# Router on rows that are not normalized, and a row copy shared by two engines

## The chip, the core and the metric

The kernel runs on one core of one Trainium2 chip. The metric is the device time of one execution in microseconds; the time given for a kernel is the median of its runs. All data are float32, and a float32 matmul shows as two matmul records in the trace.

## The reference

One layer of a perceiver: cross-attention of 8 x 64 tokens of width 512 on a context of 1601 rows, then a linear-attention block with an MLP, then a mixture of eight experts of which each token uses two. Each block works on layer-normalized rows and adds to the residual `x`. The part that matters here is the last block:

```python
x = x + _L0_ffn_ref(_layernorm(x, axis=-1), w_router, w0, w1, wo)

# in _L0_ffn_ref, x being the normalized rows, t tokens
router_logits = x @ w_router
top_w, top_i = jax.lax.top_k(router_logits, K)          # K = 2 of 8
top_w = jax.nn.softmax(top_w, axis=-1)
gating = zeros((t, e)).at[arange(t)[:, None], top_i].add(top_w)
for ei in range(e):
    hmid = silu(x @ w0[ei]) * (x @ w1[ei])
    out = out + gating[:, ei:ei + 1] * (hmid @ wo[ei])
```

The layer norm is (x - mean) / sqrt(var + 1e-5), with no learned scale.

## The kernel before

The 512 tokens lie as four tiles (t = 0 to 3) of 128 rows. The order of the instructions on each engine is the order in which the program states them, and each engine's queue, the DMA issues in it included, is worked off in that order. Matmul outputs go to PSUM banks of 128 x 512 from two pools of four: `mm_bank` for work that is emptied at once, `acc_bank` for sums that last. A bank is taken again in turn, when its last reader is done.

Stages: cross-attention, linear attention, MLP, routing, experts. What the change touches begins at the end of the linear attention's output. `hidden(f, tokens)` (L765) makes one block of 128 columns of the MLP's first layer; `turn_h2(t)` (L731) transposes a tile of its input, and its four evacuations take turns between DVE and ACT. The second MLP matmul is `mlp_out(t, f, hid)` (L791), one matmul of 128 x 512 that adds block f of 16 to the sum of tile t. For the first eight blocks all four tiles are done together; the last eight (`HELD`) are kept back, so that each tile can be finished by itself. `last_chunks(t, part)` (L842) issues some of these eight for one tile. They are the work that stands between the steps of the routing, which is done one tile behind:

- `finish(t)` (L826): DVE adds the sum to the residual `xs`, takes mean and variance (L830, L832), ACT takes the square root (L834), DVE its reciprocal (L835) and the normalized rows `mn` (L836). ACT's queue then stores `mn` in DRAM (L839), POOL's stores `xs` as the start of the output (L840).
- `turn_m(t)` (L848): TensorE transposes the four 128 x 128 blocks of `mn`, ACT copies the bank to `m_t` (L853).
- `route(t)` (L855): four matmuls of 128 x 8 for the logits (L859), which DVE copies (L863); then the two largest, their places, and one-hot rows `hot` and `member`.
- `rank_tile(t)` (L884): a matmul over the tokens before counts each token's place in its expert; DVE makes `rank` (L890) and `onehot` (L894), a 128 x 128 selection of the rows for expert 0.
- `first_rows(t)` (L896): four matmuls add the selected rows, already transposed, of tile t to one bank, `first_bank`.
- `count_tile(t)` (L876) keeps the running count of members; `tabulate(t)` (L908) is a chain of small DVE operations ending in `spot`, by which POOL writes a table in DRAM with two indirect DMAs (L928).

The loop at L940 goes over t = 1 to 3 and puts the steps of tile t - 1 between the last chunks of tile t. After it come the steps of tile 3, then ACT copies `first_bank` to `xg_t0` (L959), the rows of the first expert's first tile. DVE takes the count and the last two tabulations, one matmul sums the counts (L966), DVE copies them (L968), and the gates follow from the two largest logits (L971 to L981): exp of the difference, a reciprocal, and a product with the one-hot rows. ACT stores the gates beside the rows in DRAM (L982), POOL loads the table (L984).

The experts follow. For each, TensorE makes the hidden rows (L1081), DVE and ACT apply the gate function (L1044, L1046), TensorE transposes and multiplies back (L1052, L1089), ACT scales by the gate, and POOL adds the rows to the output by an indirect DMA (L1062). The rows of all tiles but the very first are fetched by POOL from DRAM (L1017), by places that DVE works out from the loaded table (L1007 to L1011). An expert with more than 128 rows takes a small second group; one with many more takes a further whole tile. Weights stream through a ring of twelve buffers of 1 MB by DMAs on SP's queue (L192).

```python
    for t in range(1, NT):
        last_chunks(t, range(0, 4))
        turn_m(t - 1)
        last_chunks(t, range(4, 5))
        route(t - 1)
        last_chunks(t, range(5, 7))
        rank_tile(t - 1)
        last_chunks(t, range(7, HELD))
        finish(t)
        first_rows(t - 1)
```

Of the kernel before, what the change touches and what calls it, by code (L numbers as in the profile page):

```python
# [15 lines left out]
F32 = mybir.dt.float32  # L16
AF = mybir.ActivationFunctionType
ALU = mybir.AluOpType
AX = mybir.AxisListType

P = 128
B, S, D = 8, 64, 512
LK = 1601
NT = B * S // P
KC = D // P
# [7 lines left out]
NE, FE = 8, 1024  # L33
# [5 lines left out]
HELD = 8  # L39
# [7 lines left out]
def perceiver_kernel(  # L47
# [22 lines left out]
    nc = tc.nc  # L70
# [4 lines left out]
    small = ctx.enter_context(tc.tile_pool(name="small", bufs=2))  # L75
# [6 lines left out]
    def mm_bank(name):  # L82
        return ps.tile([P, 512], F32, tag="mm", name=name)

    def acc_bank(name):
        return ps.tile([P, 512], F32, tag="acc", name=name)
# [10 lines left out]
    xs = resid.tile([P, NT, D], F32, name="xs")  # L97
    for t in range(0, NT, 2):
        nc.sync.dma_start(xs[:, t : t + 2, :], x[:, t : t + 2, :])
    moe = ctx.enter_context(tc.tile_pool(name="moe", bufs=1))  # L100
# [109 lines left out]
    ident = const.tile([P, P], F32, name="ident")  # L210
# [8 lines left out]
    router = col[:, 4 * KC + FF // P :].rearrange("p (c e) -> p c e", c=KC)  # L219
# [21 lines left out]
    ones = const.tile([P, P], F32, name="ones")  # L241
# [523 lines left out]
    def hidden(f, tokens):  # L765
# [4 lines left out]
        for c in range(KC):  # L770
# [5 lines left out]
                stop=(c == KC - 1),  # L776
            )

    hid_banks = {}

    hidden(0, slice(0, 3 * P))
# [9 lines left out]
    def mlp_out(t, f, hid):  # L791
        nc.tensor.matmul(  # L792
            acc[t],
            hid[:, t * P : (t + 1) * P],
            need("w2", f // 4)[:, f % 4, :],
            start=(f == 0),
            stop=(f == FF // P - 1),
        )
# [17 lines left out]
    mn = mlp.tile([P, NT, D + NE], F32, tag="mn", name="mn")  # L816
# [6 lines left out]
    member = moe.tile(full, F32, name="member")  # L823
    members = moe.tile(full, F32, name="members")

    def finish(t):  # L826

        nc.vector.tensor_tensor(xs[:, t, :], acc[t], xs[:, t, :], ALU.add)  # L828
        st = small.tile([P, 6], F32, tag="st", name=f"st_m_{t}")
        nc.vector.bn_stats(st, xs[:, t, :])  # L830
        mv = small.tile([P, 2], F32, tag="mv1", name=f"mv_m_{t}")
        nc.vector.bn_aggr(mv, st)  # L832
        rstd = small.tile([P, 1], F32, tag="rstd1", name=f"rstd_m_{t}")
        nc.scalar.activation(rstd, mv[:, 1:2], AF.Sqrt, bias=eps)  # L834
        nc.vector.reciprocal(rstd, rstd)  # L835
        nc.vector.tensor_scalar(  # L836
            mn[:, t, :D], xs[:, t, :], mv[:, 0:1], rstd, ALU.subtract, ALU.mult
        )
        nc.scalar.dma_start(mn_dram[t * P : (t + 1) * P, :D], mn[:, t, :D])  # L839
        nc.gpsimd.dma_start(out[t * P : (t + 1) * P, :], xs[:, t, :])  # L840

    def last_chunks(t, part):  # L842
        for f in part:
            mlp_out(t, nf - HELD + f, hids[nf - HELD + f])
# [3 lines left out]
    def turn_m(t):  # L848
        bank = mm_bank(f"tr_m_{t}")
        for c in range(KC):  # L850
            nc.tensor.transpose(bank[:, c * P : (c + 1) * P], mn[:, t, c * P : (c + 1) * P], ident)
        m_ts[t] = mlp2.tile([P, KC, P], F32, tag="mT", name=f"m_t_{t}")
        nc.scalar.copy(m_ts[t].rearrange("p c q -> p (c q)"), bank)  # L853

    def route(t):  # L855

        bank = mm_bank(f"router_{t}")
        for c in range(KC):
            nc.tensor.matmul(  # L859
                bank[:, :NE], m_ts[t][:, c, :], router[:, c, :], start=(c == 0), stop=(c == KC - 1)  # L860
            )
        logits = small.tile([P, NE], F32, tag="logits", name=f"logits_{t}")
        nc.vector.tensor_copy(logits, bank[:, :NE])  # L863
        nc.vector.max(out=top[:, t, :], in_=logits)
        where = small.tile([P, NE], mybir.dt.uint32, tag="where", name=f"where_{t}")
        nc.vector.max_index(out=where, in_max=top[:, t, :], in_values=logits)
        nc.vector.tensor_copy(chosen[:, t, :], where[:, :2])
        nc.vector.tensor_tensor(
            hot[:, t, :, :],
            enum[:, None, :].to_broadcast([P, 2, NE]),  # L870
            chosen[:, t, :, None].to_broadcast([P, 2, NE]),
            ALU.is_equal,
        )
        nc.vector.tensor_tensor(member[:, t, :], hot[:, t, 0, :], hot[:, t, 1, :], ALU.add)

    def count_tile(t):  # L876
        if t == 0:
            nc.vector.tensor_copy(members[:, 0, :], member[:, 0, :])
        else:
            nc.vector.tensor_tensor(members[:, t, :], members[:, t - 1, :], member[:, t, :], ALU.add)  # L880
# [3 lines left out]
    def rank_tile(t):  # L884

        bank = mm_bank(f"rank_{t}")
        if t > 0:
            nc.tensor.matmul(bank[:, :NE], ones, members[:, t - 1, :], start=True, stop=False)
        nc.tensor.matmul(bank[:, :NE], earlier, member[:, t, :], start=(t == 0), stop=True)
        nc.vector.scalar_tensor_tensor(  # L890
            rank[:, t, :], bank[:, :NE], 1.0, member[:, t, :], ALU.add, ALU.mult
        )
        onehots[t] = mlp2.tile([P, P], F32, tag="onehot", name=f"onehot_{t}")
        nc.vector.tensor_scalar(onehots[t], slot[:, :P], rank[:, t, 0:1], None, ALU.is_equal)  # L894

    def first_rows(t):  # L896

        for c in range(KC):
            nc.tensor.matmul(
                first_bank[:, c * P : (c + 1) * P],  # L900
                mn[:, t, c * P : (c + 1) * P],
                onehots[t],
                start=(t == 0 and c == 0),
                stop=(t == NT - 1),
                skip_group_check=True,
            )

    def tabulate(t):  # L908

        r = small.tile([P, 2], F32, tag="r", name=f"r_{t}")  # L910
        for k in range(2):
            mine = small.tile([P, NE], F32, tag="which", name=f"mine_{t}_{k}")
            nc.vector.scalar_tensor_tensor(
                mine, hot[:, t, k, :], 1.0, rank[:, t, :], ALU.mult, ALU.mult, accum_out=r[:, k : k + 1]
            )
        over = small.tile([P, 2], F32, tag="over", name=f"over_{t}")
        nc.vector.tensor_scalar(over, r, float(P), None, ALU.is_gt)
        for i in range(2, NI):
            nc.vector.scalar_tensor_tensor(over, r, float(i * P), over, ALU.is_gt, ALU.add)

        at = small.tile([P, 2], F32, tag="at", name=f"at_{t}")
        nc.vector.tensor_scalar(at, r, 32.0, -32.0, ALU.mult, ALU.add)
        nc.vector.scalar_tensor_tensor(at, chosen[:, t, :], 4.0, at, ALU.mult, ALU.add)
        nc.vector.scalar_tensor_tensor(
            spot[:, t, :], over, float(1 - P * NE * NI), at, ALU.mult, ALU.add
        )
        for k in range(2):
            nc.gpsimd.indirect_dma_start(  # L928
                out=table.rearrange("p k two -> (p k) two"),
                out_offset=bass.IndirectOffsetOnAxis(ap=spot[:, t, k : k + 1], axis=0),  # L930
                in_=named[:, t, :],
                in_offset=None,
                bounds_check=P * NE * NI - 1,
                oob_is_err=True,
            )

    last_chunks(0, range(HELD))
    finish(0)
    first_bank = acc_bank("first_rows")
    for t in range(1, NT):  # L940

        last_chunks(t, range(0, 4))
        turn_m(t - 1)
        last_chunks(t, range(4, 5))
        route(t - 1)
        last_chunks(t, range(5, 7))
        rank_tile(t - 1)
        last_chunks(t, range(7, HELD))
        finish(t)
        first_rows(t - 1)  # L950
        if t > 1:
            tabulate(t - 2)
        count_tile(t - 1)
    turn_m(NT - 1)
    route(NT - 1)
    rank_tile(NT - 1)
    first_rows(NT - 1)
    xg_t0 = moe.tile([P, KC, P], F32, name="xgT_first")
    nc.scalar.copy(xg_t0.rearrange("p c q -> p (c q)"), first_bank)  # L959
    count_tile(NT - 1)  # L960
    for t in range(NT - 2, NT):
        tabulate(t)
# [2 lines left out]
    bank = mm_bank("counts")  # L965
# [3 lines left out]

    e2 = moe.tile([P, NT], F32, name="e2")  # L970
    nc.vector.tensor_tensor(e2, top[:, :, 1], top[:, :, 0], ALU.subtract)  # L971
    nc.scalar.activation(e2, e2, AF.Exp)
    r1 = moe.tile([P, NT], F32, name="r1")
    nc.vector.tensor_scalar_add(r1, e2, 1.0)
# [17 lines left out]
    if True:  # L992
# [150 lines left out]
        if True:  # L1143
# [24 lines left out]
            flat = "p e i -> p (e i)"  # L1168
# [243 lines left out]
```

## Time and profile before

| what | us |
|---|---|
| median of three runs | 684.81 (684.4 to 684.9) |
| profiled execution | 685.44 |
| its span, first to last instruction | 683.7 |
| second MLP matmul (L792), 128 records, busy | 58.8 |
| last add of the MLP's sum (L828) starts | 424.42 |
| first expert matmul (L1081) starts | 435.91 |
| last scatter to the output (L1062) starts | 673.40 |

The profile gives times from the span's start. A row of the timeline is start, length, engine, line, operation, output and inputs, and in brackets how long the engine had been idle and what ended that. "PEld" is the load of weights into the array, which runs beside a matmul; "ACTq" and "SPq" are the queues' own instructions, such as the issue of a DMA. The end of a matmul is modelled: matmuls of 128 x 512 take 0.59 in the trace but follow each other every 0.43. A table by stage gives, for a stretch of time, each engine's busy time and the share of full clock that TensorE was granted.

### The profile page before, as it was taken

To read this page: it belongs to the slowest core of one execution; us is meant where nothing else is said; L and a number is where in the kernel's file an instruction comes from. 1 tells how busy PE (TensorE), PEld (TensorE's weight loads), DVE (VectorE), ACT (ScalarE), POOL (GpSimd) and SP (SyncE) were. 2 spreads that over 40 slices of the span, in tenths; PEclk is the share of its full clock that TensorE was granted. 3 is DMA by queue.
4 is the path that set the end of the run, shared out by engine and by line. 5 is a ranking of instruction groups with operands and counts; after the bars stand their busy time and mean duration, and the time that the engine had idled before them with its cause. 6 is when DMAs were issued, how large, how long until landed. Compare 5 with 4: busy or idle time off the path is not lost. (4 is left out here: it accounts for less than half of the span.)

```text
span 683.7 us, 6217 instructions
## 1 busy us (share of the span) xinstructions
PE 638.9 (93%) x2376; PEld 296.2 (43%) x2376; DVE 179.1 (26%) x403; ACT 128.2 (19%) x240; POOL 61.7 (9%) x81
## 2 busy tenths in 40 slices
PE   4998989799999999999999998898999999989993
PEld 3643434244444444445444455543444344434441
DVE  4011323132228687670000035310311101110100
ACT  2241223220132121122011200211111111111110
POOL 2000000000000000041000002331012202120000
PEclk9999999999999999999999999699999999999998
DMA  8999999999601103021311323127397595694711
GB/s 328 418 420 385 418 385 413 370 367 422 232 13 62 62 0 124 1 69 55 112 62 73 106 79 126 61 61 265 136 390 257 199 357 175 233 348 175 283 17 18
DMA packets 24222, 138.04 MB, mean 202 GB/s; under 512 B 4164, under 2 KB 4164, under 8 KB 11896
## 3 DMA queue, kind: packets, MB, share of 16 engines
q1 hardware_dynamic: 20056, 129.90, 49.0%
q0 software_dynamic: 3024, 6.58, 4.3%
q10 hardware_dynamic: 1104, 1.07, 0.4%
q8 instruction: 23, 0.38, 0.2%
q14 instruction: 15, 0.12, 0.1%
HBM read 132.56 MB, written 4.97 MB: 201 GB/s over the span
## 5 line engine op out<-in xcount | busy, mean ns | idle before, releaser
L1081 PE MATMUL up<-e_up,xgT 128*128 128x512 f32 x224 | 100.2, 595 | 1.2 <-PEq L1310 1.2
L1081 PEld LDWEIGHTS up<-e_up,xgT 128*128 128x128 f32 x224 | 40.9, 190 | 50.4 <-issue 50.4
L1089 PE MATMUL y<-e_wo,hidT 128*128 128x512 f32 x128 | 61.0, 599 | 0.0
L792 PE MATMUL mlp<-w,hid_sb 128*128 128x512 f32 x128 | 58.8, 597 | 0.0
L1046 DVE TENSOR_TENSOR mid<-up,act 128x256 f32<-128x256 f32 x35 | 14.9, 425 | 164.2 <-ACT act L1044 159.7
L771 PE MATMUL hid<-v_sb,w 128*128 128x512 f32 (+2 forms) x144 | 56.6, 545 | 0.0
L472 PE MATMUL av<-ctx,eT 128*64 128x512 f32 x192 | 48.4, 617 | 7.3 <-DMA ctx<-in_ctx_dram 6.5
L423 PE MATMUL sc<-ctxT,pw_t 128*64 128x401 f32 (+1 forms) x256 | 48.1, 501 | 0.7 <-DMA ctxT<-in_ctx_T_dram 0.7
L771 PEld LDWEIGHTS hid<-v_sb,w 128*128 128x128 f32 x144 | 26.2, 190 | 29.1 <-issue 27.3
L792 PEld LDWEIGHTS mlp<-w,hid_sb 128*128 128x128 f32 x128 | 23.4, 190 | 24.9 <-issue 24.9
L1044 ACT ACTIVATE act<-up 128x256 f32<-128x256 f32 x35 | 13.4, 383 | 104.5 <-PE up L1081 95.7
L786 POOL TENSOR_TENSOR xin<-xin,b_bc 128x512 f32<-128x512 f32 x4 | 5.1, 1263 | 295.3 <-DVE rstd_h L728 291.1
L423 PEld LDWEIGHTS sc<-ctxT,pw_t 128*64 128x64 f32 x256 | 20.3, 136 | 26.3 <-issue 22.9
L1062 POOL DMA_INDIRECT out_dram<-y_sb,dst_late x11 | 16.8, 1529 | 161.1 <-ACTq L1310 103.7
L1089 PEld LDWEIGHTS y<-e_wo,hidT 128*128 128x128 f32 x128 | 22.4, 190 | 19.5 <-issue 19.1
L595 PE MATMUL wk<-h_t,wk 128*128 128x512 f32 x64 | 29.5, 604 | 0.0
L595 PE MATMUL wq<-h_t,wq 128*128 128x512 f32 x64 | 29.4, 602 | 0.0
L532 PE MATMUL v<-wv,h_t 128*128 128x512 f32 x64 | 28.7, 597 | 0.6 <-DVE h_t L519 0.6
L472 PEld LDWEIGHTS av<-ctx,eT 128*64 128x64 f32 x192 | 13.9, 140 | 35.3 <-issue 24.6
L691 PE MATMUL wo<-wo,a_t 128*128 128x512 f32 x64 | 28.6, 597 | 0.0
L671 DVE RECIPROCAL rden<-rden 128x512 f32<-128x512 f32 x8 | 26.8, 3354 | 0.3
L828 DVE TENSOR_TENSOR xs<-mlp,xs 128x512 f32<-128x512 f32 x4 | 2.8, 692 | 87.3 <-PE mlp L792 87.3
(230 smaller groups left out, 653.1 us busy)
## 6 DMA issues: line engine op xcount, KB each, us to landing
e_up<-in_L_ffn_up_dram SPq DMA_DIRECT2D x32, 1024.0 KB, 7.9
ctx<-in_ctx_dram SPq DMA_DIRECT2D x24, 1024.0 KB, 17.4
ctxT<-in_ctx_T_dram SPq DMA_DIRECT2D x24, 802.0 KB, 15.7
e_wo<-in_L_ffn_wo_dram SPq DMA_DIRECT2D x16, 1024.0 KB, 10.0
w<-in_L_attn_w_dram SPq DMA_DIRECT2D x8, 1024.0 KB, 11.7
ctxT<-in_ctx_T_dram SPq DMA_DIRECT2D x8, 796.0 KB, 16.7
big_up<-in_L_ffn_up_dram SPq DMA_DIRECT2D x4, 1024.0 KB, 7.9
wv<-in_L_attn_wv_dram SPq DMA_DIRECT2D x2, 1024.0 KB, 13.0
```

Of the source, the lines that this page charges most:

```text
L423: nc.tensor.matmul(sc[h * S : (h + 1) * S, :width], pw_t[:, c, (2 * t + h) * S : (2 * t + h + 1) * S], keys[h][:, c, :], start=(c == 0), s ...
L472: nc.tensor.matmul(av[h * S : (h + 1) * S, :], e_t[:, 4 * g + j, h * S : (h + 1) * S], rows[h][:, j, :], start=(g == 0 and j == 0), stop=F ...
L532: nc.tensor.matmul(bank, h_t[:, c, t * P : (t + 1) * P], wv_n[:, c, :], start=(c == 0), stop=(c == KC - 1))
L595: nc.tensor.matmul(bank, w[:, c, (j % 4) * P : (j % 4 + 1) * P], h_t[:, c, :], start=(c == 0), stop=(c == KC - 1),)
L671: nc.vector.reciprocal(rden, rden)
L691: nc.tensor.matmul(wo_banks[t], a_t[:, j, t * P : (t + 1) * P], wo_r[j // 4][:, j % 4, :], start=(j == 0), stop=(j == nj - 1),)
L771: nc.tensor.matmul(hid_banks[f][:, tokens], w[:, c, (f % 4) * P : (f % 4 + 1) * P], h2_t[:, c, tokens], start=(c == 0), stop=(c == KC - 1),)
L792: nc.tensor.matmul(acc[t], hid[:, t * P : (t + 1) * P], need("w2", f // 4)[:, f % 4, :], start=(f == 0), stop=(f == FF // P - 1),)
L1046: nc.vector.tensor_tensor(hid, bank[:, FQ:], act, ALU.mult)
L1062: nc.gpsimd.indirect_dma_start(out=out, out_offset=bass.IndirectOffsetOnAxis(ap=dst[:n, :], axis=0), in_=y_sb[:n, :], in_offset=None, boun ...
L1081: nc.tensor.matmul(bank, xg_t[:, c, :], up_of[q][:, c, :], start=(c == 0), stop=(c == KC - 1))
L1089: nc.tensor.matmul(y, h_t[:, j, :], w[:, 2 * (q % 2) + j, :], start=(q + j == 0), stop=(q + j == NQ))
```

## The change

Mean and scale of the layer norm are taken out of the router's path. With m the mean and s the reciprocal deviation of a row, the normalized row times the router's weights is s * (row @ w - m * sum(w)). The sums of the router's columns are made once, by matmuls with a matrix of ones ahead of `hidden(0)`, and copied by DVE. `turn_m` transposes `xs` instead of `mn`. The logits are `router_sums * (-m) + row @ w`, without s: since s is positive, the order of a row's logits is the same, and s is multiplied into the difference of the two largest ahead of the exponential. `finish` keeps -m in `neg_mean` and s in `rstds`, for all tiles.

The order changes, too. In the loop, `turn_m` comes after two chunks instead of four, `route` after one more, `rank_tile` after two more, and three are left before `finish`. `first_rows(2)` moves out of the loop: two of its four chunks stand ahead of the last tile's transposes and two behind. The copy of `first_bank` is cut into halves of 128 x 256, one on ACT and one on DVE, the latter ahead of `count_tile` and the last tabulations on that engine.

```diff
--- before.py
+++ after.py
@@ -776,6 +776,12 @@
                 stop=(c == KC - 1),
             )
 
+
+    bank = mm_bank("router_sums")
+    for c in range(KC):
+        nc.tensor.matmul(bank[:, :NE], ones, router[:, c, :], start=(c == 0), stop=(c == KC - 1))
+    router_sums = moe.tile([P, NE], F32, name="router_sums")
+    nc.vector.tensor_copy(router_sums, bank[:, :NE])
     hid_banks = {}
 
     hidden(0, slice(0, 3 * P))
@@ -823,6 +829,9 @@
     member = moe.tile(full, F32, name="member")
     members = moe.tile(full, F32, name="members")
 
+    neg_mean = moe.tile([P, NT], F32, name="neg_mean")
+    rstds = moe.tile([P, NT], F32, name="rstds")
+
     def finish(t):
 
         nc.vector.tensor_tensor(xs[:, t, :], acc[t], xs[:, t, :], ALU.add)
@@ -830,7 +839,8 @@
         nc.vector.bn_stats(st, xs[:, t, :])
         mv = small.tile([P, 2], F32, tag="mv1", name=f"mv_m_{t}")
         nc.vector.bn_aggr(mv, st)
-        rstd = small.tile([P, 1], F32, tag="rstd1", name=f"rstd_m_{t}")
+        nc.vector.tensor_scalar(neg_mean[:, t : t + 1], mv[:, 0:1], -1.0, None, ALU.mult)
+        rstd = rstds[:, t : t + 1]
         nc.scalar.activation(rstd, mv[:, 1:2], AF.Sqrt, bias=eps)
         nc.vector.reciprocal(rstd, rstd)
         nc.vector.tensor_scalar(
@@ -848,11 +858,12 @@
     def turn_m(t):
         bank = mm_bank(f"tr_m_{t}")
         for c in range(KC):
-            nc.tensor.transpose(bank[:, c * P : (c + 1) * P], mn[:, t, c * P : (c + 1) * P], ident)
+            nc.tensor.transpose(bank[:, c * P : (c + 1) * P], xs[:, t, c * P : (c + 1) * P], ident)
         m_ts[t] = mlp2.tile([P, KC, P], F32, tag="mT", name=f"m_t_{t}")
         nc.scalar.copy(m_ts[t].rearrange("p c q -> p (c q)"), bank)
 
     def route(t):
+
 
         bank = mm_bank(f"router_{t}")
         for c in range(KC):
@@ -860,7 +871,9 @@
                 bank[:, :NE], m_ts[t][:, c, :], router[:, c, :], start=(c == 0), stop=(c == KC - 1)
             )
         logits = small.tile([P, NE], F32, tag="logits", name=f"logits_{t}")
-        nc.vector.tensor_copy(logits, bank[:, :NE])
+        nc.vector.scalar_tensor_tensor(
+            logits, router_sums, neg_mean[:, t : t + 1], bank[:, :NE], ALU.mult, ALU.add
+        )
         nc.vector.max(out=top[:, t, :], in_=logits)
         where = small.tile([P, NE], mybir.dt.uint32, tag="where", name=f"where_{t}")
         nc.vector.max_index(out=where, in_max=top[:, t, :], in_values=logits)
@@ -893,9 +906,9 @@
         onehots[t] = mlp2.tile([P, P], F32, tag="onehot", name=f"onehot_{t}")
         nc.vector.tensor_scalar(onehots[t], slot[:, :P], rank[:, t, 0:1], None, ALU.is_equal)
 
-    def first_rows(t):
-
-        for c in range(KC):
+    def first_rows(t, chunks=range(KC)):
+
+        for c in chunks:
             nc.tensor.matmul(
                 first_bank[:, c * P : (c + 1) * P],
                 mn[:, t, c * P : (c + 1) * P],
@@ -939,24 +952,29 @@
     first_bank = acc_bank("first_rows")
     for t in range(1, NT):
 
-        last_chunks(t, range(0, 4))
+        last_chunks(t, range(0, 2))
         turn_m(t - 1)
-        last_chunks(t, range(4, 5))
+        last_chunks(t, range(2, 3))
         route(t - 1)
-        last_chunks(t, range(5, 7))
+        last_chunks(t, range(3, 5))
         rank_tile(t - 1)
-        last_chunks(t, range(7, HELD))
+        last_chunks(t, range(5, HELD))
         finish(t)
-        first_rows(t - 1)
+        if t < NT - 1:
+            first_rows(t - 1)
         if t > 1:
             tabulate(t - 2)
         count_tile(t - 1)
+    first_rows(NT - 2, range(0, 2))
     turn_m(NT - 1)
+    first_rows(NT - 2, range(2, KC))
     route(NT - 1)
     rank_tile(NT - 1)
     first_rows(NT - 1)
     xg_t0 = moe.tile([P, KC, P], F32, name="xgT_first")
-    nc.scalar.copy(xg_t0.rearrange("p c q -> p (c q)"), first_bank)
+    flat = "p c q -> p (c q)"
+    nc.scalar.copy(xg_t0[:, :2, :].rearrange(flat), first_bank[:, : 2 * P])
+    nc.vector.tensor_copy(xg_t0[:, 2:, :].rearrange(flat), first_bank[:, 2 * P :])
     count_tile(NT - 1)
     for t in range(NT - 2, NT):
         tabulate(t)
@@ -969,6 +987,7 @@
 
     e2 = moe.tile([P, NT], F32, name="e2")
     nc.vector.tensor_tensor(e2, top[:, :, 1], top[:, :, 0], ALU.subtract)
+    nc.vector.tensor_tensor(e2, e2, rstds, ALU.mult)
     nc.scalar.activation(e2, e2, AF.Exp)
     r1 = moe.tile([P, NT], F32, name="r1")
     nc.vector.tensor_scalar_add(r1, e2, 1.0)
```

## What was predicted

> **What bounds the kernel now.** I read the page's busy table and slices first, then the table of busy time by stage, then the timeline of the last router tile, engine by engine.
>
> ```profile
> PE 638.9 (93%) x2376; PEld 296.2 (43%) x2376; DVE 179.1 (26%) x403; ACT 128.2 (19%) x240; POOL 61.7 (9%) x81
> PEclk9999999999999999999999999699999999999998
> ```
>
> TensorE is busy 93% of the span, and one slice of the clock row (the 6) is slow. The stage table finds it (start:end in us, its length, then busy time of PE, PEld, DVE, ACT, POOL, then clock, DMA share, GB/s):
>
> ```profile
> 412.00:420.00 8.00, 8.00 (x32) 4.27 (x30) 4.58 (x23) 0.80 (x2) 1.52 (x2) 1.00 0.21 71
> 420.00:428.00 8.00, 5.86 (x31) 3.86 (x30) 4.55 (x22) 0.41 (x3) 1.92 (x3) 1.00 0.65 235
> 428.00:436.00 8.00, 5.29 (x23) 5.04 (x23) 4.53 (x36) 1.42 (x3) 1.96 (x2) 0.50 0.24 92
> 436.00:445.00 9.00, 9.00 (x15) 3.86 (x16) 1.78 (x10) 2.87 (x4) 3.88 (x4) 0.68 0.04 2
> 445.00:684.00 239.00, 218.29 (x711) 95.39 (x709) 31.27 (x95) 34.95 (x79) 36.13 (x30) 0.99 0.58 208
> ```
>
> Through the second MLP matmul TensorE has no gap. From 425.2 it waits for the last tile's routing, its clock falls to 0.50, and the first expert's matmuls run at half clock until 441.7. Then TensorE is full again, and its waits in the expert stage are on DVE and ACT, never on a DMA. So a microsecond gained or lost before the first expert matmul is one at the end. The last tile (start, length, instruction):
>
> ```profile
> 424.42 0.69 DVE L828 TENSOR_TENSOR xs<-mlp,xs 128x512 f32<-128x512 f32 x1 [0.54 <-PE mlp L792]
> 426.62 0.55 DVE L836 TENSOR_SCALAR mn<-xs,mv_m,rstd_m 128x512 f32<-128x512 f32 x1
> 427.20 0.33 ACTq L839 DMA_DIRECT2D mn_dram<-mn  x1
> 427.22 0.66 PE L851 MATMUL tr_m<-ident,mn 128*128 128x128 f32 x4 [2.01 <-DVE mn L836]
> 427.97 0.58 ACT L853 COPY m_t<-tr_m 128x512 f32<-128x512 f32 x1 [1.58 <-PE tr_m L851]
> 428.60 1.88 PE L859 MATMUL router<-col,m_t 128*128 128x8 f32 x8 [0.73 <-ACT m_t L853]
> 432.66 0.29 DVE L894 TENSOR_SCALAR onehot<-slot,rank 128x128 f32<-128x128 f32 x1
> 433.01 2.07 PE L899 MATMUL first_rows<-onehot,mn 128*128 128x128 f32 x8 [0.58 <-DVE onehot L894]
> 435.12 0.59 ACT L959 COPY xgT_first<-first_rows 128x512 f32<-128x512 f32 x1 [6.57 <-PE first_rows L899]
> 435.64 0.16 DVE L968 COPY count<-counts 128x8 f32<-128x8 f32 x1
> 435.91 1.19 PE L1081 MATMUL up<-e_up,xgT_first 128*128 128x512 f32 x1 [0.60 <-ACT xgT_first L959]
> ```
>
> Two things to see. ACT's queue holds the store of `mn` (L839) ahead of the copy of the transposed rows (L853). And two chains end together before the first expert matmul: ACT's row copy at 435.71, and DVE's last small op, the count copy L968, at 435.80, which follows two tabulations that ran during `first_rows`. In the built order of both kernels the first `up` matmul waits for both.
>
> **What the skill says.** "TensorE: Matmul & The Clock Gate", Part 1: a free-running window of about 3.4 us halves the clock after an idle window and restores it after a busy one. The trace agrees: full clock until 428.06, half until 441.71, which is 13.65 us, four windows of 3.41; a gap near 62.8 cost exactly one. Part 4 there says that transposes hardly count as busy; consistent with 0.66 us of them not saving the window that ended at 428.06. Its specifications call ScalarE's queue strict FIFO, as L839 and L853 stand. "PSUM — Partial Sum Buffer", Terms: two engines on one bank at once is an error, so two readers must take turns. The trace has such a pair:
>
> ```profile
> 309.63 0.41 DVE L742 TENSOR_SCALAR v_sb<-tr_h,col 128x128 f32<-128x128 f32 x1 [0.75 <-PE tr_h L734]
> 310.08 0.46 ACT L738 ACTIVATE v_sb<-tr_h,col 128x128 f32<-128x128 f32 x1 [0.53 <-DVE v_sb L742]
> 310.57 0.41 DVE L742 TENSOR_SCALAR v_sb<-tr_h,col 128x128 f32<-128x128 f32 x1 [0.53 <-ACT v_sb L738]
> ```
>
> **The change part by part.**
>
> *router_sums.* Eight matmul records of 128x8 ahead of `hidden(0)`. Such records stand 0.11 us apart at full clock (the router's eight take 0.89 from 401.08), so 0.89 us. After `hidden(0)` TensorE waits for DVE's L729 until 308.94: its eight records of 384 columns end at 308.38, so 0.56 is absorbed and **+0.33** stays. The DVE copy falls in DVE's 0.75 idle before 309.63: nothing. The extra bank shifts the rotation by one; every bank taken was emptied long before.
>
> *neg_mean, rstds, logits, e2.* neg_mean fits in the 0.36 us in which DVE waits for ACT's square root. The logits op keeps its place, about 0.17 like L890, which also reads PSUM. e2's extra product (0.16) comes after the count copy, beside the first expert's matmuls. Nothing. Without the cover of the square root, 0.2 per tile.
>
> *Earlier transposes in the loop.* For t = 1, let 0 be the end of tile 0's last matmul issue (396.35: eight records of 0.43 before 399.78). Now two chunks end at 1.71 and the transposes at 2.15, which no longer wait for `mn`. But ACT's order is unchanged: square root, store of `mn`, copy. The store is issued when L836 is done and ends at 399.75, so 3.40. The copy (0.58) therefore runs from 3.43 to 4.01, and the router can start at 4.09; its one covering chunk ended at 2.15 + 0.86 = 3.01. TensorE waits 1.08 where it waited nothing; about 0.1 of gap before `first_rows` goes. **+0.98.** For t = 2 and 3 the previous `first_rows` (0.89) stands in front: chunk ends at 3.90, router at 4.08, so 0.18 each, against gaps of 0.1 and 0.15 that go: **+0.08 and +0.03**. If the store held ACT for less than its 0.35, 0.3 of the 0.98 goes; below that nothing. Bounds for the loop: +0.7 to +1.3. Sum at the start of the last tile's `first_rows(2)`: **+1.42**.
>
> *The tail*, with 0 at that start (424.15 before). The add starts at 0.27, ends 0.96; the transposes run at 1.02 between two halves of `first_rows(2)`, 2.05 earlier than before (3.07). Then the store again: issued 3.05 to 3.38, since `mn` is not sooner; copy 3.42 to 4.00, against 3.82 to 4.40: only **-0.39**. The filler ends at 2.1, so TensorE still waits two microseconds. The router starts at 4.06. If the clock is still full it takes 1.07 to the logits instead of 1.92: **-0.85**. I take this, as a window opened at about 2 would end at 5.5; but the window from there holds 0.37 busy, mostly 8-column matmuls, against 0.36 in the window before the fall at 428.06, 0.33 before the one at 62.8, and 0.44 in the emptiest that kept its clock (127.7 to 131.1). So the fall comes after the router, and `first_rows(3)` still costs its 2.07 cold (1.05 warm). Member, rank, onehot as before: onehot ends at 7.59, `first_rows(3)` at 9.72.
>
> *The split copy.* TensorE signals once, after the last of the four chunks, so ACT's half can't start early. Both halves read one bank, so DVE's waits for ACT's: 0.04 + 0.37 (ACT's 128x256 copies) + 0.03 + 0.41 (DVE's) = 0.85 against 0.63: rows ready at 10.57, 0.2 slower by itself. Worse is what is queued behind DVE's half: the member count, both tabulations, the count copy. Before, they ran during `first_rows`; from 432.87 to 435.80, 2.93 us (2.7 without one 0.40 op). Now they start when DVE's copy leaves, 10.49, and end at 13.42. The `counts` matmul waits for the member count, too, but is long done. First `up` at 13.52 against 11.76: **+1.76**. By steps: -0.39 -0.85, and 3.70 from the end of `first_rows` to the count copy where it was 0.72, **+2.98**.
>
> *Clock after that.* Before, 5.8 us of `up` ran cold (435.91 to 441.71), a loss of 2.9. Now TensorE idles some 3.5 us before them but for `counts`, so they start cold; release needs one full window: 3.4 to 6.8 us cold, a loss of 1.7 to 3.4. I take no difference, -1.2 to +0.5 as bounds.
>
> *Moved queues.* POOL's table writes for tiles 2 and 3 are fed 3 us later, each 2.4 us after the last; `late` lands about 2 us later (448.1 before), and its reader on DVE stands behind `mid` L1046 at 450.0, itself 3 later. SP's and ACT's other entries keep their order. Nothing.
>
> **Sum.** 1.42 + 1.76 = +3.2; without the slow op some +2.95. I take **+3.1**. The profiled execution took 685.44 (span 683.7 and 1.7 around it), 0.6 above the median of 684.81; against that median the forecast is **687.9**.
>
> **Rivals.**
> - A: the clock falls later, `first_rows(3)` is warm: onehot to end 1.05, `up` at 12.50, +0.74; sum +2.2: **687.0** (685.8 with a short cold stretch). For it: windows there hold about 0.42 busy, near the kept 0.44.
> - B: it falls before the router, if a window happens to open just at 0.5 to 1.0, in the gap: +0.85 more, +4.0: **688.8**.
> - C: the count copy is not what the first `up` waits for. Then `up` starts at the rows' copy, 10.6, the tail gives -1.1, and the sum is +0.3: **685.1**. For it: the trace names ACT as releaser. Against: the order, and `up`'s weight load at 435.88 follows the count copy (435.80) by less than the row copy (435.71).
> - D, the other side: the filler keeps TensorE's clock full throughout. It decides if no window between 425 and 438 holds less than the threshold, between 0.36 and 0.44 busy. Then `up` starts as in A and nothing is cold: +2.2 - 2.9 = -0.7, **684.1**, not slower; with the store not holding ACT too (0.3 in the loop, 0.35 in the tail), 683.5. Against: the longest wait, for the tabulations, is now longer than a window.
>
> **How the numbers follow.** Forecast 0.50; A 0.20; B 0.12; C 0.07; D 0.08; something faster still 0.03. 0.2% (1.4 us) is about what a measurement of this kernel can tell. Slower by more: forecast, B and most of A, 0.78. Within: C, most of D and the lucky end of A, 0.16. Faster: 0.06. The range takes the forecast with its clock bounds, A, B and C's upper half: **685.1 to 689.3**.
>
> **What would show it.** In the new profile: the first tile's router waiting about 1 us for ACT's copy, with the store just ahead of it; the last copy only 0.4 sooner after its add; DVE's half of the rows starting when ACT's ends; two tabulations between it and the count copy; the first `up` right behind the count copy, 13 to 14 us after `first_rows(2)` starts, at clock 0.50. It is wrong if `up` starts before the count copy, or the clock stays at 1.00 there.

## The result, and the profile after

The changed kernel took 689.94 us (median of 6 runs, 688.44 to 690.6) where the kernel before took 684.96 in the same session (6 runs, 684.4 to 686.98). The ratio of the runs is 1.006, with a 95% interval of 1.0049 to 1.0072: 3.4 to 4.9 us slower. (The two medians lie 5.0 apart, just outside that interval; the ratio is used from here on.) The profiled execution took 688.44, with a span of 686.7.

The page of the changed kernel, its busy table and clock row:

```profile
PE 639.0 (93%) x2384; PEld 296.2 (43%) x2384; DVE 180.9 (26%) x410; ACT 128.0 (19%) x240; POOL 61.4 (9%) x81
PEclk9999999999999999999999999699999999999998
```

Nothing has changed on this level: eight more matmul records, one slow slice. The table of busy time by stage of the changed kernel (same columns as before) shows where TensorE has less to do:

```profile
412.00:420.00 8.00, 7.96 (x33) 4.35 (x32) 4.23 (x21) 0.88 (x2) 0.54 (x1) 1.00 0.16 61
420.00:428.00 8.00, 7.11 (x33) 4.34 (x32) 3.84 (x15) 0.29 (x1) 2.67 (x3) 1.00 0.52 174
428.00:436.00 8.00, 3.95 (x20) 3.47 (x20) 3.49 (x22) 1.31 (x3) 1.96 (x2) 0.68 0.47 163
436.00:445.00 9.00, 6.78 (x10) 3.22 (x11) 4.20 (x34) 1.14 (x2) 2.91 (x3) 0.52 0.04 2
```

Before, TensorE was busy for all 9.00 us of the last stretch; now for 6.78, with more of DVE beside it (4.20 against 1.78). Its wait has moved to the stretch in which the first expert matmuls should already run. Two places in the timeline of the changed kernel explain it. The first is the second tile's round (t = 1), with the first tile's router in it:

```profile
397.61 0.60 PE L861 MATMUL tr_m<-ident,xs 128*128 128x128 f32 x4
398.04 1.02 PE L798 MATMUL mlp<-w,hid_sb 128*128 128x512 f32 x2
398.94 0.35 ACTq L849 DMA_DIRECT2D mn_dram<-mn  x1
399.32 0.58 ACT L863 COPY m_t<-tr_m 128x512 f32<-128x512 f32 x1 [1.20 <-DVE mn L846]
399.96 0.39 PE L870 MATMUL router<-col,m_t 128*128 128x8 f32 x2 [0.90 <-ACT m_t L863]
```

The transposes end at 398.21, and ACT had been idle 1.20 us ahead of the copy. Yet the copy starts at 399.32, right behind the issue of the store of `mn`. What ended ACT's wait is DVE's L846, the very op that the change meant to take out of the router's path: the copy doesn't read `mn`, but the store ahead of it on ACT does. In the kernel before, the store stood there too, but the transposes ended after it, and the router (no bracket) did not keep TensorE waiting:

```profile
399.40 0.35 ACTq L839 DMA_DIRECT2D mn_dram<-mn  x1
399.78 0.60 PE L851 MATMUL tr_m<-ident,mn 128*128 128x128 f32 x4
400.42 0.58 ACT L853 COPY m_t<-tr_m 128x512 f32<-128x512 f32 x1 [1.83 <-PE tr_m L851]
401.08 1.04 PE L859 MATMUL router<-col,m_t 128*128 128x8 f32 x8
```

The second place is the last tile of the changed kernel:

```profile
425.40 0.61 PE L912 MATMUL first_rows<-onehot,mn 128*128 128x128 f32 x4
425.67 0.69 DVE L837 TENSOR_TENSOR xs<-mlp,xs 128x512 f32<-128x512 f32 x1 [2.04 <-PE mlp L798]
426.42 0.66 PE L861 MATMUL tr_m<-ident,xs 128*128 128x128 f32 x4 [0.41 <-DVE xs L837]
427.87 0.55 DVE L846 TENSOR_SCALAR mn<-xs,mv_m,rstds 128x512 f32<-128x512 f32 x1
428.45 0.33 ACTq L849 DMA_DIRECT2D mn_dram<-mn  x1
428.62 0.17 DVE L930 TENSOR_SCALAR over<-r 128x2 f32<-128x2 f32 x1
428.87 0.58 ACT L863 COPY m_t<-tr_m 128x512 f32<-128x512 f32 x1 [1.23 <-DVE over L930]
429.51 1.06 PE L870 MATMUL router<-col,m_t 128*128 128x8 f32 x8 [1.99 <-ACT m_t L863]
...
432.81 0.29 DVE L907 TENSOR_SCALAR onehot<-slot,rank 128x128 f32<-128x128 f32 x1
433.15 2.07 PE L912 MATMUL first_rows<-onehot,mn 128*128 128x128 f32 x8 [0.58 <-DVE onehot L907]
435.26 0.37 ACT L976 COPY xgT_first<-first_rows 128x256 f32<-128x256 f32 x1 [5.80 <-PE first_rows L912]
435.67 0.42 DVE L977 COPY xgT_first<-first_rows 128x256 f32<-128x256 f32 x1 [2.57 <-ACT xgT_first L976]
437.24 0.16 DVE L937 SCALAR_TENSOR_TENSOR spot<-over,at 128x2 uint32<-128x2 f32 x1
438.48 0.16 DVE L937 SCALAR_TENSOR_TENSOR spot<-over,at 128x2 uint32<-128x2 f32 x1
438.56 0.16 DVE L986 COPY count<-counts 128x8 f32<-128x8 f32 x1
438.63 0.16 DVE L989 TENSOR_TENSOR e<-top 128x4 f32<-128x4 f32 x1
438.82 1.19 PE L1100 MATMUL up<-e_up,xgT_first 128*128 128x512 f32 x1 [2.00 <-issue]
```

Read it from the bottom. The first `up` matmul starts 0.10 after the count copy ends (438.72), although its rows had been ready since 436.09. The bracket says "issue": the profile attributes no releaser to it. The subtraction for the gates (L989), which doesn't touch what `up` needs, ends closer still, at 438.79; that `up` waits for the count copy and not for it is shown below, by the experiment that moves the count copy ahead of the tabulations and leaves the subtraction behind them. Between the rows and the count copy stand the two tabulations, each ending in an L937. Above that, DVE's half of the rows waits for ACT's half ("<-ACT xgT_first L976"), having stood idle for 2.57 us during `first_rows`, in which DVE used to tabulate. Further up, the bracket of `m_t`'s copy names L930, a step of a tabulation that ended at 428.79, a little after the store's issue (428.78). The copy needs neither; the experiment that moves the store leaves the tabulation where it is and tells them apart.

### The profile page after: what moved, and what is told of

It is laid out like the page before. It is cut to its first block, busy times and chain, and to the rows that moved or that the text cites. A ratio compares the mean times of both kernels' runs of the same rounds, so it can differ in the third digit from the quotient of the medians.

```text
span 686.7 us, 6240 instructions
## 1 busy us (share of the span) xinstructions
PE 639.0 (93%) x2384; PEld 296.2 (43%) x2384; DVE 180.9 (26%) x410; ACT 128.0 (19%) x240; POOL 61.4 (9%) x81
## 3 DMA queue, kind: packets, MB, share of 16 engines
q10 hardware_dynamic: 1104, 1.07, 0.4%
```

## The experiments

Each was timed beside the kernel before, whose median was 685.13 (40 runs) beside the first four, 685.71 (33 runs) beside the next four, and 685.03 (11 runs) beside the last two. Differences in us are the ratio's interval, less one, times that median. "The interval from `first_rows`" is the time from the start of the last tile's `first_rows(2)` to the first `up`, 11.76 before and 13.42 after. "The loop" is the time from the last `tr_h` (L734 before) to that `first_rows(2)`, 115.21 and 116.86. Both are read from one execution of each kernel.

**One copy again.** The changed kernel, with the rows copied by ACT alone.

```diff
-    nc.scalar.copy(xg_t0[:, :2, :].rearrange(flat), first_bank[:, : 2 * P])
-    nc.vector.tensor_copy(xg_t0[:, 2:, :].rearrange(flat), first_bank[:, 2 * P :])
+    nc.scalar.copy(xg_t0.rearrange("p c q -> p (c q)"), first_bank)
```

> The changed kernel with one edit undone: ACT copies the whole first_rows bank again, nothing of it stands in DVE's queue. My theory (the tail is lost because the tabulations and the count copy queue behind DVE's half): the tabulations run during first_rows again, the count copy ends within 0.2 us of ACT's copy, the first up matmul comes some 3.0 us sooner after first_rows(2) starts (10.4 instead of 13.4), and the time is 2 to 4 us below the changed kernel, depending on where the clock is released: 685 to 687.5. Rival (the waits in the loop and the clock are the loss; the tabulations are hidden either way): no more than 0.3 us below the changed kernel.

Measured: 686.56 (15 runs), ratio 1.0018 (1.0009 to 1.0028), so +0.6 to +1.9 us. The loop took 116.88, as in the changed kernel, and the interval from `first_rows` 10.49. The timeline of its last tile:

```profile
434.40 2.07 PE L912 MATMUL first_rows<-onehot,mn 128*128 128x128 f32 x8 [0.58 <-DVE onehot L907]
436.51 0.59 ACT L975 COPY xgT_first<-first_rows 128x512 f32<-128x512 f32 x1 [5.80 <-PE first_rows L912]
436.84 0.16 DVE L984 COPY count<-counts 128x8 f32<-128x8 f32 x1
437.14 1.22 PE L1098 MATMUL up<-e_up,xgT_first 128*128 128x512 f32 x1 [0.45 <-ACT xgT_first L975]
```

With DVE free during `first_rows`, the count copy comes 0.4 after it instead of 3.3, and `up` follows the rows. The split costs the tail 13.42 - 10.49 = 2.93 us, most of the change's loss. The runs agree: the interval of the ratio lies wholly below the changed kernel's (1.0049 to 1.0072).

**The split alone.** The kernel before, with only its row copy replaced by the two halves.

```diff
-    nc.scalar.copy(xg_t0.rearrange("p c q -> p (c q)"), first_bank)
+    flat = "p c q -> p (c q)"
+    nc.scalar.copy(xg_t0[:, :2, :].rearrange(flat), first_bank[:, : 2 * P])
+    nc.vector.tensor_copy(xg_t0[:, 2:, :].rearrange(flat), first_bank[:, 2 * P :])
```

> The kernel before with one edit of the change alone: the copy of first_rows in halves, ACT's and DVE's, the latter ahead of the count and the tabulations. My theory: DVE's half starts when ACT's ends, the count copy ends 3.7 us after first_rows instead of 0.7, so 3.0 us slower than before: about 688. Rival: the halves run side by side and the time falls by about 0.2 us, or the tabulations are hidden and it stays the same.

Measured: 687.66 (9 runs), ratio 1.0036 (1.0021 to 1.0052), +1.4 to +3.6 us. The loop is untouched (115.21) and the interval from `first_rows` is 14.58, which is 2.82 more than before. Half of what that costs came back where `up` ran at half clock for only 3.00 us instead of 5.80. The same price of the interval from both directions: it belongs to the split and not to its company.

**The former order in the loop.** The changed kernel, with the chunks of the loop where they were, so that `xs` is transposed as late as `mn` used to be.

```diff
-        last_chunks(t, range(0, 2))
+        last_chunks(t, range(0, 4))
         turn_m(t - 1)
-        last_chunks(t, range(2, 3))
+        last_chunks(t, range(4, 5))
         route(t - 1)
-        last_chunks(t, range(3, 5))
+        last_chunks(t, range(5, 7))
         rank_tile(t - 1)
-        last_chunks(t, range(5, HELD))
+        last_chunks(t, range(7, HELD))
```

> The changed kernel with the former places of the steps in the loop (transposes after four chunks, router after one more, rank after two more). My theory (with the earlier places the router waits for ACT's copy, which stands behind the store of mn): the waits of 0.9, 0.45 and 0.2 us ahead of the router are gone, the three rounds of the loop take 1.7 us less, the tail is unchanged, so 1.7 us below the changed kernel. Rival (the router waits for something of the new data path, not of the order): the waits stay and so does the time.

Measured: 687.74 (7 runs), ratio 1.0043 (1.0028 to 1.0059), +1.9 to +4.0 us. The loop is back at 115.16, so all of its loss comes from the earlier transposes. This is read from the traces: in the runs the interval overlaps that of the changed kernel (1.0049 to 1.0072), and no gain on it is shown. The tail of this execution is not that of the changed kernel, though. The last router in its timeline:

```profile
427.88 1.88 PE L870 MATMUL router<-col,m_t 128*128 128x8 f32 x8 [1.99 <-ACT m_t L863]
```

1.88 instead of 1.06: here the clock fell at 427.58, before the router, and the interval from `first_rows` was 14.23. This is the prediction's rival B, in another kernel. Part of that came back in `up`, of which only 3.24 us ran at half clock instead of 5.79. The tail's program is that of the changed kernel; what it costs depends on when the clock falls.

**The store behind the copy.** The changed kernel, with the store of `mn` issued on ACT after `m_t`'s copy.

```diff
     def finish(t):
-        nc.scalar.dma_start(mn_dram[t * P : (t + 1) * P, :D], mn[:, t, :D])
     def turn_m(t):
         nc.scalar.copy(m_ts[t].rearrange("p c q -> p (c q)"), bank)
+        nc.scalar.dma_start(mn_dram[t * P : (t + 1) * P, :D], mn[:, t, :D])
```

> The changed kernel with ACT's store of mn issued after the copy of the transposed rows instead of ahead of it; the loop keeps its new order. My theory: the copy then starts as soon as the transposes are done, so the waits ahead of the router in the loop vanish (1.5 us), and in the tail the copy starts 1.7 us sooner, at 1.8 instead of 3.5 after first_rows(2) starts; all behind it follows, and the time falls by some 3.2 us, by more if the clock stays full longer. Rival (ACT's copy waits for the engine or a buffer, not for the store's place): the copy starts where it did, no change.

Measured: 687.28 (22 runs), ratio 1.0031 (1.0021 to 1.0041), +1.4 to +2.8 us. The loop took 115.15, again the former value, with the earlier transposes in place, and the interval of the ratio lies below that of the changed kernel. The timeline of its last tile:

```profile
427.57 0.56 ACT L862 COPY m_t<-tr_m 128x512 f32<-128x512 f32 x1
427.89 0.55 DVE L846 TENSOR_SCALAR mn<-xs,mv_m,rstds 128x512 f32<-128x512 f32 x1
428.18 1.06 PE L870 MATMUL router<-col,m_t 128*128 128x8 f32 x8 [0.64 <-ACT m_t L862]
428.47 0.33 ACTq L863 DMA_DIRECT2D mn_dram<-mn  x1
429.67 0.22 DVE L874 SCALAR_TENSOR_TENSOR logits<-router_sums,neg_mean,router 128x8 f32<-128x8 f32 x1
```

Now the copy runs ahead of `mn`, and the router waits 0.64 instead of 1.99: this is the change as it was meant. The tabulation's L930 runs at 428.65, after the copy has begun, so it was the store that held the copy. It starts at 2.15 after `first_rows(2)`, not at the 1.8 expected, because the square root (427.36, 0.29 long) stands ahead of it on ACT. The router starts 1.35 us sooner after `first_rows(2)`, but only 0.97 of it reaches `up`: the logits op starts 1.49 after the router, against a router of 1.06, because tile 1's tabulation stands ahead of it on DVE. Loop and tail together gain 2.68 of the 3.2 expected.

**Both repairs**, the edits of the first and the fourth experiment together.

> The changed kernel with both repairs: one row copy on ACT, and the store of mn behind the copy of the transposed rows. My theory: the two add up, since one lies in the loop and ahead of the router, the other behind first_rows. First up matmul 9.7 us after first_rows(2) starts (11.8 before, 13.4 in the changed kernel, 10.5 and 12.4 with one repair each); against the kernel before that is 2.1 gained less 0.4 for the router sums, so about 683.3, give or take 1 for where the clock is released. Rival (they hide the same wait): no better than the better of the two, 686.5.

Measured: 684.32 (17 runs), ratio 0.9978 (0.9967 to 0.9989), 0.8 to 2.3 us faster than before. Loop 115.16, interval from `first_rows` 9.53. In the traces, one execution each, the two repairs add up: loop and tail together are 130.28 in the changed kernel, 2.91 less with the first, 2.68 less with the second, 5.59 less with both. The former order isn't needed.

**The count copy ahead of the tabulations**, on top of both repairs. Tile 1's tabulation moves behind the last `onehot`, and the last two behind the count copy.

```diff
-        if t > 1:
+        if 1 < t < NT - 1:
             tabulate(t - 2)
...
     count_tile(NT - 1)
-    for t in range(NT - 2, NT):
-        tabulate(t)
+    tabulate(NT - 3)
...
     nc.vector.tensor_copy(count, bank[:, :NE])
+    for t in range(NT - 2, NT):
+        tabulate(t)
```

> As e5_both, and DVE's order behind the last router is changed: tile 1's tabulation goes behind the last onehot instead of ahead of the last logits, and the count copy goes ahead of the last two tabulations. My theory: the last logits no longer queue behind a tabulation (0.4 us), and the first up matmul waits for ACT's copy alone, at 9.3 instead of 9.7 after first_rows(2) starts: about 682.9. Rival: the table's writes, fed later, come late for the fetches of the second expert, and the time is above that of e5_both.

Measured: 684.18 (16 runs), ratio 0.9981 (0.9972 to 0.9991). In the trace the interval is 8.32 where 9.3 was expected:

```profile
432.64 0.59 ACT L975 COPY xgT_first<-first_rows 128x512 f32<-128x512 f32 x1 [4.97 <-PE first_rows L912]
432.87 0.17 DVE L983 COPY count<-counts 128x8 f32<-128x8 f32 x1 [0.46 <-PE counts L981]
433.28 9.81 PE L1099 MATMUL up<-e_up,xgT_first 128*128 128x512 f32 x16 [0.45 <-ACT xgT_first L975]
435.68 0.16 DVE L988 TENSOR_TENSOR e<-top 128x4 f32<-128x4 f32 x1
```

`up` now starts right behind ACT's copy (433.23), 2.40 ahead of the subtraction L988, which stayed behind the tabulations. So it was the count copy that held it in the changed kernel. The interval is 1.2 shorter than with both repairs, but some 0.8 of that is luck: the clock fell 6.92 after `first_rows(2)` here, 4.18 there, so that the last rank matmul and `first_rows(3)` took 0.39 and 1.45 instead of 0.59 and 2.08. Of the gain, 0.3 is given back by a half-clock stretch of 5.43 us instead of 4.89 in `up`. Against the kernel with both repairs, whose ratio's interval overlaps almost entirely, no difference is shown in the runs.

**Dummy matmuls, in the kernel before.** They write a bank that nobody reads, and keep TensorE busy in the gaps of the last tile.

```diff
+    fill_bank = acc_bank("fill")
+    def fill(n, cols=512):
+        for _ in range(n):
+            nc.tensor.matmul(fill_bank[:, :cols], ident, xs[:, 0, :cols], start=True, stop=True)
...
+    fill(2)
     turn_m(NT - 1)
+    fill(1, 256)
     route(NT - 1)
+    fill(1)
     rank_tile(NT - 1)
+    fill(1, 256)
     first_rows(NT - 1)
...
     nc.tensor.matmul(bank[:, :NE], ones, members[:, NT - 1, :], start=True, stop=True)
+    fill(1, 256)
```

> The kernel before with six dummy matmuls (of 512 and 256 columns, into a bank that nobody reads) in TensorE's gaps of the last tile: work is added, none is taken away. It measures what the fall of the clock costs. If the clock stays at 1.00, router 0.85, first_rows 1.0 and the first expert 1.7 to 3.4 us are gained, less at most 0.5 of dummies in the way: 680.5 to 682. If the windows count something else, or the dummies only push the work back, 685 to 686.5.

Measured: 683.01 (6 runs), ratio 0.9956 (0.9944 to 0.9969), 2.1 to 3.8 us faster. Its table by stage, and its first `up` in the timeline:

```profile
425.00:431.00 6.00, 5.26 (x28) 3.46 (x28) 3.72 (x17) 0.88 (x2) 1.60 (x2) 1.00 0.71 264
431.00:436.00 5.00, 3.63 (x20) 2.33 (x19) 3.80 (x32) 1.67 (x2) 1.97 (x2) 1.00 0.03 8
436.00:445.00 9.00, 8.99 (x23) 4.17 (x24) 2.57 (x12) 2.46 (x5) 3.57 (x4) 1.00 0.04 2
```

```profile
436.01 7.10 PE L1092 MATMUL up<-e_up,xgT_first 128*128 128x512 f32 x16 [1.08 <-DVE e L982]
```

The clock stays at 1.00 in all three stretches. With `first_rows` at full speed (1.16 instead of 2.07), `up` then waits 1.08 for DVE. The bracket names the subtraction L982, which stands behind the tabulations and the count copy; by the experiment above the count copy (ends 435.76) is the likelier, though `up` follows it by 0.25 here and by 0.10 in the changed kernel. Either way DVE's queue holds `up` again: the faster engine uncovers the next wait. So the half clock of the tail, in a kernel that is otherwise unchanged, is worth these 2.1 to 3.8 us with that new wait already taken off.

**Dummy matmuls in the repaired kernel** (with the count copy first; five, of which the one ahead of the transposes has 256 columns where there were two of 512).

> As e6_count_first with five dummy matmuls in the gaps that are left in the last tile. With the clock kept, first_rows (1.0) and the first expert (1.7 to 3.4) run at full speed: about 679. If the clock falls nonetheless, 683 to 684.

Measured: 682.07 (5 runs), ratio 0.9951 (0.9938 to 0.9964). About 679 was expected; this is a miss, though the clock held and the interval from `first_rows` is 8.11. The timeline of the expert stage has two waits of TensorE that were not there before, and ACT's table load ahead of the first:

```profile
439.00 1.28 ACT L1073 ACT_TABLE_LOAD   x1 [3.01 <-DMA mn_dram<-mn]
...
441.24 0.41 PE L1081 MATMUL ht<-ident,mid 128*128 128x128 f32 x2 [0.87 <-issue]
...
455.00 1.13 PE L1064 MATMUL xgt<-ident,xg 128*128 128x128 f32 x8 [0.67 <-DMA xg<-mn_dram,src_late]
```

`up` is now done so early that the table for the gate's activation function is late (it is loaded only when the activation's turn comes, behind a wait for the store of the gates), and 1.28 us of load stand in the path to `mid` and `ht`. The Trainium skill, "ScalarE: Activation LUTs", What ACT_TABLE_LOAD costs, gives about 1283 ns for the load, and the trace agrees. The drain of about 1380 ns that the page adds to each switch doesn't show: in the kernel before, a load starts 0.01 after ACT's row copy ends (435.71), and the activation behind it starts 0.01 after the load (437.00). The second wait is for rows that the late tables of POOL point to: in none of the traces above does this `xgt` wait for `xg`.

**The table loaded early**, by a one-column activation of the same function right behind the issue of the gates' store.

```diff
+    warm3 = small.tile([P, 1], F32, tag="warm3", name="warm3")
+    nc.scalar.activation(warm3, eps, AF.Silu)
```

> As e8_fill_best, with ACT's table for the gate function loaded right after the gates are stored, by a dummy activation, instead of behind the wait of the first expert's first activation. My theory: with the clock kept, the first expert's first transposes wait 0.87 us because that table (1.28 us) is loaded only when the store of the gates has landed; loaded sooner, the wait goes, and the time falls by 0.7 to 0.9 us against e8_fill_best, to about 681.3 beside a kernel before of 685.7. Rival (the store's landing itself is what ACT waits for): nothing gained.

Measured: 682.38 (6 runs), ratio 0.996 (0.9947 to 0.9973), no better than without it (0.9938 to 0.9964). A miss: the wait of `ht` is gone, but what it yielded is spent one step later, as the timeline shows:

```profile
456.43 1.14 PE L1066 MATMUL xgt<-ident,xg 128*128 128x128 f32 x8 [1.35 <-DMA xg<-mn_dram,src_late]
```

**The table of tile 1 sooner.** The same, with tile 1's tabulation back in the loop, so that POOL's chain of writes starts earlier.

```diff
-        if 1 < t < NT - 1:
+        if t > 1:
             tabulate(t - 2)
...
-    tabulate(NT - 3)
```

> As e9_gate_table with tile 1's tabulation back ahead of the last logits. My theory: POOL's chain of table writes starts some 3 us sooner, the wait for the fetched rows of the second expert (0.67 us) goes, and the last logits are 0.4 us later: within 0.3 us of e9_gate_table. Rival: the writes are bound by one another and not by their feeding, the fetch waits as before, and the time is 0.4 us above e9_gate_table.

Measured: 680.69 (6 runs), ratio 0.994 (0.9925 to 0.9955), 3.1 to 5.1 us faster than before: the lowest ratio of all, and a miss on the good side. Its median is 1.7 below that of the kernel it was made from, timed beside it, but the two intervals overlap. POOL issues the load of `late` at 446.03 instead of 448.29 in the first kernel with dummies and repairs, and `xgt` no longer waits. The interval from `first_rows` is 0.4 longer (8.48) than in that first kernel, as was expected for the tabulation ahead of the last logits. The clock is again 1.00 from 425 to 445.

## Why the prediction was right, and where its sizes were off

The sign and the mechanism were right, and the forecast's size was low: +3.1 us, where the ratio's interval gives +3.4 to +4.9. The measured median, 689.94, lies 0.6 above the top of the range; the ratio, put on the median that the forecast was built on (684.81), gives 688.9, inside it.

| step | forecast | trace |
|---|---|---|
| router_sums (last `wo` group to `tr_h(3)`) | +0.33 | 5.20 - 4.84 = +0.36 |
| loop, t = 1 | +0.98 | 9.58 - 8.51 = +1.07 |
| loop, t = 2 | +0.08 | 10.08 - 9.62 = +0.46 |
| loop, t = 3 | +0.03 | 9.84 - 9.67 = +0.17 |
| tail to the first `up` | +1.76 | 13.42 - 11.76 = +1.66 |
| sum to the first `up` | +3.2 | +3.7 |

- *router_sums*: right.
- *The loop*: right in its cause, shown from two sides: with the former order 115.16, with the store behind the copy 115.15, before 115.21. Mis-sized is the term for **t = 2**, 0.46 instead of 0.08, which makes most of the shortfall. There the copy starts at 409.19, while the transposes were done at 408.68 and the store's issue ended at 408.85; that is 0.34 behind the store, where it was 0.03 for t = 1 and 0.09 for t = 3. Since the loss goes with the store's place, it belongs to the store; why it held this one copy longer stays open.
- *The tail*: by the sum of the steps within 0.1 (they add to 1.74 in the prediction, 1.76 by its end points). The copy ran at 3.47 after the start of `first_rows(2)` (forecast 3.42), the router at 4.11, at full clock, which fell 5.56 after that start (about 5.5). That the fall came where it was taken to come is luck: with the same tail it came at 3.81 in the kernel with the former loop, and in the other kernels without dummies between 3.91 and 6.92. `onehot` ended at 7.70, not 7.59. The logits op took 0.22, not 0.17.
- *The split copy*: right, and the largest term. DVE's half starts 0.04 after ACT's ends; 0.37 + 0.04 + 0.42 is 0.83 for a copy that ACT alone does in 0.59. From the end of `first_rows` to the end of the count copy 3.50 (forecast 3.70). The single copy gave back 2.93, and the split alone cost 2.82.
- *Clock after that*: 5.79 us of `up` at half clock, against 5.80; no difference, as taken. This is luck as well: in the other kernels without dummies it was 3.00 to 5.99.
- *POOL*: its load of `late` was issued at 447.85 instead of 446.09 and was waited for by nobody. The cover was thin: the first two kernels with repairs and dummies uncovered it.

Of the rivals, A and D didn't come about (the clock fell, between router and `first_rows(3)`). C is out: with the rows ready at 436.09, `up` waited for the count copy. B's early fall did occur, in the kernel with the former loop. The bracket on which D rested, that a window falls somewhere between 0.36 and 0.44 busy, doesn't hold in later traces (last section).

The traced +3.7 lies inside the ratio's interval, so the runs don't show that a term is missing from the sum. The two profiled executions lie only 3.0 apart: the one after reached its last `wo` group, ahead of anything that was changed, 0.76 sooner (303.34 against 304.10), and from the first `up` to the end it took 247.9 where the one before took 247.8. Such differences between executions have one source that is shown in the last section; that it makes up these 0.76 isn't shown.

## What to carry to other kernels

Taking an operation out of a value's path gains little while another instruction that needs the same operation stands ahead on the same queue. Here the DMA issue of a store held a copy that no longer depended on its data: the last router started 4.11 after `first_rows(2)` instead of 4.45, and with one line moved, 2.76. Splitting a short copy over two engines lost here on two counts: the halves of one PSUM bank took turns, and the second engine's queue of small operations was on the path. Halves in two banks, or DVE's half behind its small operations, were not tried. And each repair uncovers the wait behind it (count copy, function table, late table), so the next ones are to be looked for in the new trace rather than in the old.

## What the runs showed of the hardware

The clock's half-speed stretches last multiples of 3.41 us (3.41, 6.83, 10.24, 13.65) in every trace, apart from the one that runs past the last instruction, but where their boundaries lie, counted from the span's start, differs between executions: modulo 3.413, at 1.40 before, 0.89 after, and 1.92, 2.27, 0.92 and 0.14 in the first four experiments. The Trainium skill, "TensorE: Matmul & The Clock Gate", Part 1, says that the window is free-running and doesn't reset with the kernel, so that the cost varies between runs; the traces agree. Its effect is visible in a part of the program that no kernel here alters, the cross-attention. The same two stretches in the table by stage, of the kernel before:

```profile
62.90:66.20 3.30, 3.30 (x10) 0.90 (x8) 0.00 (x0) 0.21 (x2) 0.00 (x0) 0.50 1.01 414
128.30:131.60 3.30, 2.02 (x10) 0.77 (x12) 0.00 (x0) 0.98 (x2) 0.00 (x0) 1.00 1.01 318
```

and of the changed kernel with one copy:

```profile
62.90:66.20 3.30, 2.90 (x14) 0.85 (x10) 0.36 (x1) 0.00 (x0) 0.00 (x0) 1.00 1.02 420
128.30:131.60 3.30, 3.03 (x8) 1.00 (x10) 0.00 (x0) 0.20 (x2) 0.00 (x0) 0.50 0.98 335
```

In the first the clock (third column from the end) is halved in the stretch from 62.9 and full in that from 128.3; in the second it is the other way round. With the store behind the copy it fell in part of both stretches (0.68 and 0.73). The 40 runs of one unaltered kernel range from 682.73 to 686.91, so that a difference of a microsecond needs many runs.

What decided a fall was less than a whole window idle, but it isn't the busy share either. Of the 3.41 us just ahead of the fall in the last tile, TensorE was busy 36% (424.64 to 428.06, before) and 38% (427.55 to 430.96, after), but also 48% in the kernel with the count copy first (428.47 to 431.88) and 64% with the store behind the copy (426.80 to 430.21), while the kernel before kept its clock after one of 44% (127.68 to 131.10). An estimate from the records orders the last tile better: 128 columns follow each other every 0.11 us, so the columns of all matmuls but the transposes fill 2 to 19% of each window there that was followed by a fall, and 24% or more of each that wasn't. This orders the windows of the last tile alone; no threshold follows from it. A few dummy matmuls of 256 and 512 columns were enough to keep 1.00 throughout the last tile.
